# A planned two-layer graph network: leaky rectifier and row scaling to ScalarE, layer-norm scalars to GpSimd, a new table of places

## The chip, the core and the metric

The kernel runs on one core of a Trainium2 chip. The metric is the device time of one execution in microseconds (us); less is better. The core has TensorE (PE in the profile), VectorE (DVE), ScalarE (ACT), GpSimd (POOL) and SyncE (SP), which here issues every DMA. Each engine works through its own list of instructions in the order in which the program gives them, and the engines wait for each other through semaphores.

## The reference

For each of 64 graphs with 256 nodes and 256 features two layers are computed, in f32:

```python
# layer 0: eight heads, four relations
attn = softmax(q @ k^T / sqrt(32))
out  = sum over r of ((attn * (adj == r)) @ (src @ Wv[r] + bv[r]))
x    = LN(src + out @ Wo + bo)
x    = LN(x + gelu(x @ W1 + b1) @ W2 + b2)
# layer 1: two graph-attention steps, then a feed-forward block
e    = leaky_relu(Wh @ a_left + (Wh @ a_right)^T, 0.2)      # 256 x 256
att  = softmax(where(adj > 0, e, -9e15), axis=1)            # over the query nodes
h    = att @ Wh                                             # done twice: W1, a1, then W2, a2
x    = LN(x + h)
x    = LN(x + relu(x @ w_ff1 + b_ff1) @ w_ff2 + b_ff2)
```

LN(v) = (v - mean) / sqrt(var + 1e-5) * gain + shift. There are four layer norms and two graph-attention steps (A and B below) in each graph.

## The kernel before

A graph is cut into 215 named steps (`Graph.operations`). A table `PLACES` gives each a place on a time axis. Graph g's step is emitted at place + 60 g, all steps of all graphs are sorted by that number, and the program is written in this order by hand (`manual_schedule`). So the table decides the order of each engine's list and nothing else: an instruction runs as soon as its engine reaches it and what it waits for has come. About seven graphs are in work at once. In the steady state the order of an engine is read by sorting its steps by their place modulo 60.

The steps that the change and the prediction touch, by name:

- `load`, `xT`, `qk0/1`, `qkc0/1`: the graph's input, the query and key products (PE, line 470) and their copies (ACT).
- `s0/1`, `maxmh`, `expmh`, `recmh`, `nrmmh`: scores (PE, L505), row maximum (DVE, L510), exponential (ACT, L518), reciprocal of its sum (DVE, L523), division by it (ACT, L528), for half m and head h.
- `eTmh`, `eWmh`, `eRmh`: transposition of the weights in 32x32 squares (DVE, L296) and a way through DRAM that puts the squares into place (SP's DMAs, L301 and L305). `ecmh` copies the result to PSUM (ACT, L536), `pmmh` multiplies it with three relation masks (DVE, L540), `plmh` with the fourth (POOL, L545). `v..`, `vc..` are the value products and their bias (PE L489, DVE L496), `po0/1` the products with the masked weights (PE, L557), `oT0/1` their copies (ACT, L563), `wo` and `ya` the output product and its residual.
- `aT aW aR` and `bT bW bR`: the same way through DRAM for the two feed-forward blocks; `hT hW hR` for layer 1's input (L317). `au0..3`, `bu0..3` are the first products (PE, L377), `ax`, `bx` their Gelu and Relu (ACT, L385). The second product is done in seven part products `ad1..7`, `bd1..7` (PE, L412), for which `aS`, `bS` make differences (POOL, L400) and `ae`, `be` add the results to the residual (DVE, L420).
- `st rt nb ln` with 1 to 4: a layer norm. `st` takes mean and variance (DVE, L337 and L339) and adds epsilon to the variance (DVE, L341, tile `ve`). `rt` raises it to the power -1/2 (POOL, L345, tile `rs`). `nb` is -mean * rs (DVE, L349). `ln` applies both (ACT, L354). `lg` and `lb` are gain and shift (POOL, L321 and L324).
- `ga0/1`, `gac0/1`: Wh and the two score vectors (PE L587, ACT L593). Then for A and for B: `ip` spreads the left scores over a PSUM tile (PE, L599), `z` adds the right score as a bias (ACT, L606), `zl` is the leaky rectifier (DVE, L610), `zm` writes the mask (DVE, L613), `zx` is the maximum (DVE, L617), `ze` the exponential and its sum (ACT, L622), `zd` divides Wh's rows by the sum (DVE, L628 for the reciprocal and L630 for two multiplications). `h10/h11` (L636) and `h2` (L650) are the products with the weights, `h1c0/1` their copies (ACT, L642), `h2a` the residual (DVE, L654).

Most matmul results share one PSUM pool with two buffers (`ps_mm`, the tiles that `mm_tile` gives): qk, v, po, wo, ga, ip, h1, h2, au, bu, and the bank of part products 2, 3 and 4. So the second next group of matmuls can't begin before a buffer has been emptied. Part products 1, 5, 6 and 7 of both feed-forward blocks share another single bank. The transposed weights that come back from DRAM have three buffers, the `z` tiles two.

Of the kernel before, what the change touches and what calls it, by code (L numbers as in the profile page):

```python
# [9 lines left out]
F32 = mybir.dt.float32  # L10
# [3 lines left out]
AF = mybir.ActivationFunctionType  # L14
ALU = mybir.AluOpType
AX = mybir.AxisListType

P = 128
S = 32
A = P // S  # L20
EPS = 1e-5
ALPHA = 0.2
# [3 lines left out]

PERIOD = 60.0
PLACES = {
    "load": 40.36, "cast": 58.74, "xT": 60.44, "qk0": 70, "qkc0": 71.44, "qk1": 87.85, "s0": 89.53,
    "qkc1": 91.95, "max01": 94.22, "max03": 94.25, "max02": 94.39, "exp01": 95.36, "rec01": 97.24,  # L30
    "exp03": 106.64, "exp02": 109.12, "jT": 113.27, "max00": 114.1, "exp00": 118.89, "rec02": 119.85,
    "nrm01": 120.5, "rec00": 121.94, "mask0": 122.78, "rec03": 123.27, "eT01": 124.55, "s1": 124.66,
    "mask1": 124.91, "nrm02": 125.88, "max11": 126.34, "v00": 126.75, "nrm03": 126.97, "eT02": 128.02,
    "vc00": 128.34, "nrm00": 128.91, "eW01": 131.85, "eR01": 133.5, "mask2": 134.22, "max13": 137.47,
    "eT03": 137.69, "eW02": 138.09, "max10": 139.15, "exp13": 140.04, "max12": 141.09, "eR02": 141.63,
    "v01": 142.38, "exp11": 142.41, "eT00": 142.98, "exp12": 143.77, "rec11": 143.99, "exp10": 144.12,
    "vc01": 146.63, "rec12": 146.73, "mask3": 146.81, "rec10": 147.48, "nrm11": 148.13, "eW03": 148.24,
    "ec01": 149.05, "eW00": 151.36, "rec13": 152.13, "eT11": 152.55, "nrm12": 153.62, "nrm13": 153.65,
    "eR00": 153.67, "eT12": 155.05, "v10": 155.72, "eW11": 155.83, "y": 156.64, "pm01": 156.67,
    "vc10": 157.33, "ec00": 158.45, "pl00": 159.54, "pl02": 160.62, "pm00": 161.31, "eR03": 162.29,  # L40
    "nrm10": 163.21, "ec02": 163.47, "v11": 164.04, "vc11": 164.08, "mask4": 164.38, "pm02": 164.4,
    "pl01": 165.26, "ec03": 167.13, "eT10": 167.24, "eW12": 168.06, "eR11": 169.25, "pl03": 169.3,
    "pm03": 173.29, "eR12": 174.65, "eW10": 176.2, "eT13": 176.62, "eR10": 177.38, "po0": 181.21,
    "ec11": 181.79, "oT0": 183.85, "pm11": 184.85, "ec10": 187.85, "pl10": 187.87, "pl12": 191.61,
    "pm10": 191.97, "pl11": 192.4, "yb": 193.93, "eW13": 195.61, "eR13": 196.93, "ec12": 197.13,
    "pm12": 199.06, "pl13": 199.85, "ec13": 202.51, "pm13": 205.64, "po1": 215.6, "oT1": 217.97,
    "wo": 219.51, "ya": 223.88, "st1": 228.47, "rt1": 233.65, "nb1": 233.99, "ln1": 238.78, "aT": 240.73,
    "ag": 245.39, "aW": 246.11, "ar": 246.93, "aR": 249.98, "au0": 253.28, "ax0": 255.01, "au1": 255.12,
    "ax1": 256.29, "au2": 257.32, "au3": 258.21, "ax2": 258.83, "ax3": 259.91, "ad1": 260.54, "aS1": 262.22,
    "ae1": 262.56, "ad5": 262.62, "ad2": 263.26, "aS2": 263.54, "aS3": 264.31, "ad3": 264.44, "ad7": 265.04,  # L50
    "aS4": 265.78, "ad4": 265.92, "ad6": 267.49, "ae5": 269.57, "ae7": 270.4, "ae": 270.63, "ae6": 271.84,
    "st2": 272.17, "rt2": 272.17, "nb2": 273.67, "ln2": 274.48, "lg2": 276.04, "lb2": 279.25, "hT": 280.72,
    "hW": 284.48, "hR": 287.09, "ga0": 291.2, "ga1": 292.43, "gac0": 295.5, "gac1": 295.79, "ipA": 296.6,
    "zA": 298, "zlA": 298.97, "zmA": 299.01, "zxA": 299.7, "zeA": 303.47, "zdA": 304.35, "h10": 304.89,
    "h1c0": 305.16, "h11": 306.57, "h1c1": 306.58, "ipB": 307.84, "zB": 308.32, "zlB": 309.79,
    "zmB": 309.85, "zxB": 311.38, "zeB": 311.5, "zdB": 318.17, "h2": 319.09, "h2a": 319.31, "st3": 322.4,
    "rt3": 324.85, "nb3": 325.29, "ln3": 325.64, "bT": 326.01, "bW": 326.15, "bR": 335.32, "bu0": 339.02,
    "bg": 339.45, "bx0": 339.7, "br": 344.42, "bu1": 345.17, "bx1": 346.89, "bu2": 347.56, "bx2": 348.07,
    "bS1": 349.24, "bu3": 349.7, "bd1": 350.78, "bx3": 352.33, "bS2": 355.82, "bd2": 356.22, "bd5": 356.9,
    "bd3": 357.53, "bS4": 358.73, "bd4": 360.41, "be5": 361.74, "be": 361.79, "bS3": 367.41, "bd6": 368.29,  # L60
    "be1": 372.14, "be6": 374.71, "bd7": 376.99, "be7": 378.33, "st4": 407.09, "rt4": 408.17, "nb4": 413.39,
    "ln4": 428.85, "lg4": 434.13, "lb4": 437.94, "store": 455.81,
}
LOAD_PLACE, LOAD_STEP = 62.0, 3.0
FFA_PLACE, GAT_PLACE, FFB_PLACE = 196.0, 200.0, 252.0

# [11 lines left out]
def kernel(  # L80
# [12 lines left out]
    nc = tc.nc  # L93
# [7 lines left out]
    C = N // P  # L101
# [8 lines left out]
    small = ctx.enter_context(tc.tile_pool(name="small", bufs=6))  # L110
# [15 lines left out]
    nhalf = const.tile([P, 2], F32, name="nhalf")  # L126
# [10 lines left out]
    def weight(w, name, mixed=False):  # L137

        k, n = w.shape[0] // P, w.shape[1]
        t = const.tile([P, k, n], F32, name=name)  # L140
        if mixed:
            mixed_rows(t, w)
        else:
            loads.append((t, w.rearrange("(k p) n -> p k n", p=P)))
        return t
# [13 lines left out]
    def rowvec(v, n, name):  # L159
        t = const.tile([P, n], F32, name=name)  # L160
        loads.append((t, _row(v, n)))
        return t
# [30 lines left out]
    scale = 1.0 / math.sqrt(DH)  # L193
# [4 lines left out]
    wo, bo_r = weight(Wo, "wo"), rowvec(bo, D, "bo_r")  # L198
# [127 lines left out]
    class Norm:  # L326
# [5 lines left out]
        def stats(self, y):  # L332
            self.y, name = y, self.name
            st = small.tile([P, C, 6], F32, tag="st", name=f"st_{name}")
            self.mv = small.tile([P, C, 2], F32, tag="mv", name=f"mv_{name}")
            for c in range(C):
                nc.vector.bn_stats(st[:, c, :], y[:, c, :])  # L337
            for c in range(C):
                nc.vector.bn_aggr(self.mv[:, c, :], st[:, c, :])  # L339
            self.ve = small.tile([P, C], F32, tag="ve", name=f"ve_{name}")  # L340
            nc.vector.tensor_scalar(self.ve, self.mv[:, :, 1], EPS, None, op0=ALU.add)  # L341

        def root(self):
            self.rs = small.tile([P, C], F32, tag="rs", name=f"rs_{self.name}")
            nc.gpsimd.tensor_tensor(self.rs, self.ve, nhalf, ALU.pow)  # L345

        def offset(self):
            self.nb = small.tile([P, C], F32, tag="nb", name=f"nb_{self.name}")
            nc.vector.scalar_tensor_tensor(self.nb, self.mv[:, :, 0], -1.0, self.rs, op0=ALU.mult, op1=ALU.mult)  # L349

        def apply(self):
            for c in range(C):
# [69 lines left out]
    class Graph:  # L422
# [179 lines left out]
        def gat_scores(self, right, name):  # L602

            self.z = bp.tile([P, C, N], F32, tag="z", name=f"{name}_z", bufs=2)
            for c in range(C):
                nc.scalar.activation(self.z[:, c, :], self.ps["left"], AF.Identity,  # L606
                                     bias=self.w[:, c, right:right + 1])

        def gat_leaky(self):
            nc.vector.scalar_tensor_tensor(self.z, self.z, ALPHA, self.z, op0=ALU.mult, op1=ALU.max)  # L610

        def gat_mask(self):
            nc.vector.copy_predicated(self.z.rearrange("p c (i n) -> p i c n", i=C), self.no, negc[:, :, None, None].to_broadcast([P, C, C, P]))  # L613
# [11 lines left out]
        def gat_divide(self, cols, name):  # L625

            rden = small.tile([P, C], F32, tag="grden", name=f"{name}_rden")
            nc.vector.reciprocal(rden, self.gden)  # L628
            for c in range(C):
                nc.vector.tensor_scalar(self.w[:, c, :cols], self.w[:, c, :cols], rden[:, c:c + 1], None,  # L630
                                        op0=ALU.mult)

        def second_product(self, ic):
            p = self.ps["h1", ic] = mm_tile([P, D + 2], f"h1_ps{self.g}_{ic}")
# [24 lines left out]
        def operations(self):  # L659

            g, ops = self.g, {}
# [58 lines left out]
            for n, right, name in (("A", D + 2, f"ga{g}"), ("B", D, f"gb{g}")):  # L720
                ops[f"ip{n}"] = lambda right=right, name=name: self.left_product(right + 1, name)
                ops[f"z{n}"] = lambda right=right, name=name: self.gat_scores(right, name)
                ops[f"zl{n}"] = self.gat_leaky
                ops[f"zm{n}"] = self.gat_mask
                ops[f"zx{n}"] = lambda name=name: self.gat_maximum(name)
                ops[f"ze{n}"] = lambda name=name: self.gat_exponential(name)
                ops[f"zd{n}"] = lambda right=right, name=name: self.gat_divide(min(right, D + 2), name)
# [12 lines left out]
    for g in range(B):  # L740
        ops = Graph(g).operations()
# [34 lines left out]
```

## Time and profile before

| | us |
|---|---|
| median of 3 runs | 3729.13 (3727.47 to 3731.34) |
| the profiled execution's own time | 3730.06 |
| its span, first to last instruction | 3728.3 |
| busy: PE, DVE, POOL, ACT | 3525.8, 3253.6, 2683.8, 2476.3 |
| one period of the steady state (one graph in, one graph out) | 56.00 |

The page gives busy times of engines, the groups of instructions with their mean duration in ns and the idle time before them, and the chain of work that ended last: going back from the last instruction, at each step to what released it. A queue that is on this chain sets the time; other idle time costs nothing. The period is read from the chain in order of time, which repeats itself: the part product that follows the two additions on DVE begins at 2025.49 us and again at 2081.49 us.

### The profile page before, as it was taken

What the parts mean: (1) busy time and instruction counts of PE and PEld (TensorE: products, weight loads), DVE (VectorE), ACT (ScalarE), POOL (GpSimd) and SP (SyncE); (2) the same over time, 40 slices, a digit from 0 to 9 for tenths busy, and PEclk for the clock granted to TensorE, in tenths of its full rate; (3) what the DMA queues carried; (4) which work ended last, traced back from release to release, by engine and by line L of the source; (5) the groups of instructions that cost most, each with busy time, mean ns of one, the idle gap of its engine ahead of it and who ended that gap; (6) DMA issues with size and microseconds to landing.
All of it is one profiled execution on the core that took longest, in us unless ns stands there. A gap on an engine that the chain in (4) does not pass through costs nothing.

```text
span 3728.3 us, 72927 instructions
## 1 busy us (share of the span) xinstructions
PE 3525.8 (95%) x25944; PEld 2739.0 (73%) x25944; DVE 3253.6 (87%) x5652; ACT 2476.3 (66%) x6661; POOL 2683.8 (72%) x2246
## 2 busy tenths in 40 slices
PE   5899999999999999999999999999999999999986
PEld 3577777777777777777777777777777777777775
DVE  4789999999999999999999999989989989989963
ACT  4667667667667666666666666666666666666642
POOL 2577777777777777777777777777777777777753
PEclk7999999999999999999999999999999999999998
DMA  6444444444444444444444444444444444444420
GB/s 176 123 127 123 120 132 123 121 131 124 122 131 124 122 131 124 122 131 124 122 131 124 122 129 124 124 128 124 124 128 124 125 128 123 126 128 123 120 77 29
DMA packets 809883, 457.93 MB, mean 123 GB/s; under 512 B 334256, under 2 KB 718896, under 8 KB 809520
## 3 DMA queue, kind: packets, MB, share of 16 engines
q1 hardware_dynamic: 809520, 453.27, 41.5%
q8 instruction: 206, 3.38, 0.4%
q14 instruction: 157, 1.29, 0.1%
HBM read 243.42 MB, written 201.33 MB: 119 GB/s over the span
## 4 chain that ended last, share of the span: by engine, by line
PE 77%; DVE 16%; ACT 2%; DMA 2%; issue 1%; SPq 1%; POOL 0%; ACTq 0%; POOLq 0%; DVEq 0%
PE po L557 12%; PE ffb_ps L377 11%; PE v_ps L489 9%; PE ffa_ps L377 6%; PE ffa_po L412 5%; PE ffb_po L412 5%; PE ffa_pq L412 5%; PE ffb_pq L412 4%; PE s L505 4%; PE h_ps L636 4%; PE ga_wps L587 3%; PE h_ps L650 3%; DVE pm L540 3%; PE qk_ps L470 3%; PE wo_ps L577 3%; DVE gb_z L610 3%
## 5 line engine op out<-in xcount | busy, mean ns | idle before, releaser
L540 DVE TENSOR_TENSOR pm<-rel,pe 128x1536 f32<-128x1536 uint8 x512 | 886.6, 1732 | 9.8 <-ACT pe L536 7.7
L545 POOL TENSOR_TENSOR pl<-rell,eT 128x512 f32<-128x512 bf16 x512 | 589.4, 1167 | 117.9 <-DMA eT<-eT_d 98.9
L345 POOL TENSOR_TENSOR rs_x<-ve_x,nhalf 128x2 f32<-128x2 f32 x256 | 182.5, 713 | 550.4 <-DVE ve_x L341 549.9
L489 PE MATMUL v_ps<-wv,xT 128*128 128x512 f32 x1024 | 491.3, 602 | 0.4 <-DVE v L496 0.4
L518 ACT ACTIVATE e<-s,nmax 128x256 f32<-128x256 f32 x1024 | 473.1, 477 | 20.8 <-DVE nmax L510 12.7
L377 PEld LDWEIGHTS ffb_ps<-ffb_T,f 128*128 128x128 f32 x2048 | 391.3, 191 | 121.6 <-issue 71.6
L377 PE MATMUL ffb_ps<-ffb_T,f 128*128 128x256 f32 x2048 | 466.7, 381 | 13.8 <-DMA ffb_T<-ffb_T_d 13.8
L377 PE MATMUL ffa_ps<-ffa_T,w 128*128 128x256 f32 x2048 | 466.5, 381 | 1.5 <-ACT ffa_h L385 1.5
L528 ACT ACTIVATE e<-e,rden 128x256 f32<-128x256 f32 x1024 | 457.1, 507 | 8.7 <-DVE rden L523 8.7
L377 PEld LDWEIGHTS ffa_ps<-ffa_T,w 128*128 128x128 f32 x2048 | 386.4, 191 | 52.5 <-ACT ffa_h L385 2.1
L557 PE MATMUL po<-pm,v 128*32 128x256 f32 x6144 | 366.3, 385 | 18.4 <-DVE pm L540 18.4
L536 ACT COPY pe<-eT 128x512 f32<-128x512 f32 x512 | 307.0, 600 | 113.6 <-DVE rden L523 93.9
L385 ACT ACTIVATE ffb_h<-ffb_ps,bf_c 128x256 f32<-128x256 f32 x512 | 215.1, 471 | 239.2 <-PE ffb_ps L377 239.2
L296 DVE STREAM_TRANSPOSE eT_sq<-e 128x512 f32<-128x512 f32 x512 | 358.2, 700 | 12.0 <-DMA eT_d<-eT_sq 10.9
L510 DVE TENSOR_REDUCE nmax<-s 128x2 f32<-128x512 f32 x512 | 336.8, 679 | 7.2 <-PE s L505 7.2
L462 POOL TENSOR_SCALAR rel<-adT 128x512 uint8<-128x512 bf16 x192 | 310.1, 1624 | 0.0
L557 PEld LDWEIGHTS po<-pm,v 128*32 128x32 f32 x6144 | 188.5, 110 | 164.0 <-issue 25.2
L385 ACT ACTIVATE ffa_h<-ffa_ps,b_c 128x256 f32<-128x256 f32 x512 | 208.0, 473 | 144.4 <-PE ffa_ps L377 124.0
L489 PEld LDWEIGHTS v_ps<-wv,xT 128*128 128x128 f32 x1024 | 185.5, 191 | 159.6 <-issue 151.5
L400 POOL TENSOR_TENSOR ffa_t<-ffa_h,ffa_t 128x512 f32<-128x512 f32 x128 | 162.9, 1272 | 178.1 <-ACT ffa_h L385 178.1
L496 DVE TENSOR_TENSOR v<-v_ps,bv_r 128x512 f32<-128x512 f32 x256 | 173.4, 677 | 65.4 <-PE v_ps L489 65.3
L420 DVE TENSOR_TENSOR ffa_res<-ffa_po,ffa_res 128x256 f32<-128x256 f32 (+2 forms) x256 | 134.2, 524 | 91.4 <-PE ffa_po L412 86.8
(141 smaller groups left out, 8054.4 us busy)
## 6 DMA issues: line engine op xcount, KB each, us to landing
eT_d<-eT_sq SPq DMA_DIRECT2D x512, 256.0 KB, 3.1
eT<-eT_d SPq DMA_DIRECT2D x512, 256.0 KB, 2.9
xin<-in_x_dram SPq DMA_DIRECT2D x256, 64.0 KB, 3.4
adi<-in_adj_dram SPq DMA_DIRECT2D x64, 256.0 KB, 3.1
y<-in_x_dram SPq DMA_DIRECT2D x64, 256.0 KB, 4.4
ffa_T_d<-ffa_T_sq SPq DMA_DIRECT2D x64, 256.0 KB, 2.0
ffa_T<-ffa_T_d SPq DMA_DIRECT2D x64, 256.0 KB, 2.7
hT_d<-hT_sq SPq DMA_DIRECT2D x64, 256.0 KB, 3.1
```

The costliest lines, as they stand in the source:

```text
L296: nc.vector.transpose(self.sq.rearrange("p a c k y -> p (c k) a y"), src.rearrange("p c (k a x) -> p (c k) a x", k=KD, a=A))
L377: nc.tensor.matmul(p[:, f - f0, :], self.wa[:, k, f * P:(f + 1) * P], self.x.nodes(k), start=(k == 0), stop=(k == KD - 1))
L385: nc.scalar.activation(self.h[half][:, f1 + f, :], self.ps[f0][:, f, :], self.func, bias=self.ba[:, f0 + f:f0 + f + 1])
L412: nc.tensor.matmul(self.p[bank][:, k], a[:, f], seven[self.name[:3]][i][:, f], start=(f == 0), stop=(f == KF // 2 - 1))
L462: nc.gpsimd.tensor_scalar(t.rearrange("p b c k y -> p (c k) b y"), self.adT.rearrange("p c k (b y) -> p (c k) b y", b=A), float(r), None, ...
L489: nc.tensor.matmul(p, self.xT[:, k, jc * P:(jc + 1) * P], wv[:, k, m].rearrange("p r n -> p (r n)"), start=(k == 0), stop=(k == KD - 1))
L510: nc.vector.tensor_reduce(self.nmax[m, h], self.s4[m][h].rearrange("p (c n) -> p c n", c=C), AX.X, ALU.max, negate=True)
L518: nc.scalar.activation(e[:, ic, :], self.s4[m][h][:, ic * N:(ic + 1) * N], AF.Exp, bias=self.nmax[m, h][:, ic:ic + 1], accum_out=self.den[ ...
L528: nc.scalar.activation(e[:, ic, :], e[:, ic, :], AF.Copy, scale=self.rden[m, h][:, ic:ic + 1])
L540: nc.vector.tensor_tensor(self.pm[m, h], self.rel.rearrange("p r b c k y -> p r (b c k y)"), bc(self.pe[m, h], [P, R - 1, C * N]), ALU.mult)
L545: nc.gpsimd.tensor_tensor(self.pm_l[m, h], self.rel_l.rearrange("p b c k y -> p (b c k y)"), self.et[m, h].t.rearrange("p b c k y -> p (b ...
L557: nc.tensor.matmul(po[hp, :], self.v[m][:, jc, r, hp], w, start=(r == 0 and jc == 0), stop=(r == R - 1 and jc == C - 1))
```

## The change

The leaky rectifier of both graph-attention steps becomes ScalarE's function Prelu with a slope of 0.2, in the instruction that added the bias; the steps `zlA` and `zlB` are gone, which leaves 213 names. The multiplications of `zd` go from DVE to ACT; its reciprocal stays on DVE. In the layer norms the addition of epsilon moves from `st` on DVE to `rt` on POOL, and `nb` from one instruction on DVE to two on POOL. All places are new, the loading of the weights included; the period of the table stays 60.

```diff
 PLACES = {
...
 }
-LOAD_PLACE, LOAD_STEP = 62.0, 3.0
-FFA_PLACE, GAT_PLACE, FFB_PLACE = 196.0, 200.0, 252.0
+LOAD_PLACE, LOAD_STEP = 122.0, 3.0
+FFA_PLACE, GAT_PLACE, FFB_PLACE = 255.0, 262.0, 264.0
...
                 nc.vector.bn_aggr(self.mv[:, c, :], st[:, c, :])
-            self.ve = small.tile([P, C], F32, tag="ve", name=f"ve_{name}")
-            nc.vector.tensor_scalar(self.ve, self.mv[:, :, 1], EPS, None, op0=ALU.add)
 
         def root(self):
             self.rs = small.tile([P, C], F32, tag="rs", name=f"rs_{self.name}")
-            nc.gpsimd.tensor_tensor(self.rs, self.ve, nhalf, ALU.pow)
+            nc.gpsimd.tensor_scalar(self.rs, self.mv[:, :, 1], EPS, None, op0=ALU.add)
+            nc.gpsimd.tensor_tensor(self.rs, self.rs, nhalf, ALU.pow)
 
         def offset(self):
             self.nb = small.tile([P, C], F32, tag="nb", name=f"nb_{self.name}")
-            nc.vector.scalar_tensor_tensor(self.nb, self.mv[:, :, 0], -1.0, self.rs, op0=ALU.mult, op1=ALU.mult)
+            nc.gpsimd.tensor_tensor(self.nb, self.mv[:, :, 0], self.rs, ALU.mult)
+            nc.gpsimd.tensor_scalar(self.nb, self.nb, -1.0, None, op0=ALU.mult)
...
-                nc.scalar.activation(self.z[:, c, :], self.ps["left"], AF.Identity,
+                nc.scalar.activation(self.z[:, c, :], self.ps["left"], AF.Prelu, alpha=ALPHA,
                                      bias=self.w[:, c, right:right + 1])
-
-        def gat_leaky(self):
-            nc.vector.scalar_tensor_tensor(self.z, self.z, ALPHA, self.z, op0=ALU.mult, op1=ALU.max)
...
             for c in range(C):
-                nc.vector.tensor_scalar(self.w[:, c, :cols], self.w[:, c, :cols], rden[:, c:c + 1], None,
-                                        op0=ALU.mult)
+                nc.scalar.activation(self.w[:, c, :cols], self.w[:, c, :cols], AF.Copy, scale=rden[:, c:c + 1])
```

The steady order that the two tables give on the engines, sorted by place modulo 60 (before begins at `po0`, after at `h2`; DVE and ACT only in the stretches that the prediction reads):

```
PE before:  po0 s1 h10 h11 v00 ipB bd6 qk0 au0 au1 bd7 au2 au3 h2 ad1 v01 ad5 ad2 ad3 ad7 ad4 ad6 qk1 s0 po1
            v10 bu0 wo v11 bu1 bu2 bu3 bd1 ga0 ga1 bd2 ipA bd5 bd3 bd4
PE after:   h2 ad1 v01 qk1 ad5 ad2 ad3 ad6 ad4 ad7 v10 po1 s0 v11 bu0 wo bu1 bu2 bu3 bd1 ga0 ga1 bd5 ipA
            bd2 bd3 po0 bd4 v00 h10 s1 h11 bd6 ipB qk0 au0 au1 bd7 au2 au3
DVE before: zlB zmB zxB pm10 be1 be6 | h2a max12 st3 ae1
DVE after:  be5 max11 zmB zxB be6 | h2a st3 ae1 vc01 | ae6 ae rec11 rec12 ae5 ae7 st2 rec10 eT11 pm01 vc10 vc11
            hT pm02 ya max00 st4 pm00 st1 pm03 eT10 eT12 max01 max02 be1 zmA zxA aT max03 eT13 zdA(reciprocal)
ACT after:  ln2 oT1 | nrm12 nrm10 ec00 bx1 nrm13 exp00 bx2 ec03 bx3 gac0 gac1 ln1 zA exp01 exp02 zeA zdA oT0
            exp03 | h1c0 nrm01 h1c1 nrm02 zB nrm00 qkc0 zeB ax0 ec10 ax1 zdB ax2
POOL after: rt2 nb2 lg2 lb2 pl02 pl01 pl00 mask0 bg br bS1 rt4 pl03 rt1 nb1
SP after:   eW03 eR03 eW11 hW hR eR11
```

| distance in the table | before | after |
|---|---|---|
| `load` to `qk0` | 29.6 | 50.4 |
| `qk0` to `bd7`, the last PE step | 307.0 | 305.6 |
| `bd7` to `store` | 78.8 | 88.8 |

## The prediction

> **What bounds the kernel now.** First the page: span and busy times.
>
> ```profile
> span 3728.3 us, 72927 instructions
> PE 3525.8 (95%) x25944; PEld 2739.0 (73%) x25944; DVE 3253.6 (87%) x5652; ACT 2476.3 (66%) x6661; POOL 2683.8 (72%) x2246
> ```
>
> PE is busiest, but DVE is near it. Then the windows of two neighbouring periods, to see whether the state is steady (columns: window, length, busy us of PE, PEld, DVE, ACT, POOL, clock):
>
> ```profile
> 2024.79:2080.79 56.00, 54.32 (x404) 42.36 (x404) 50.82 (x89) 38.55 (x105) 41.97 (x35) 1.00 0.42 125
> 2080.79:2136.79 56.00, 54.32 (x404) 42.36 (x404) 50.93 (x89) 38.56 (x105) 41.98 (x35) 1.00 0.43 126
> ```
>
> It repeats every 56.00 us at full clock. Then the chain in order of time (start, us, what), where PE loses its lead once a period:
>
> ```profile
> 2072.35 1.72 PE v_ps L489 x4
> 2074.06 0.23 PE gb_ips L599 x2
> ...
> 2074.38 0.85 ACT gb_z L606 x2
> ...
> 2075.25 1.70 DVE gb_z L610
> ...
> 2076.97 0.81 DVE gb_z L613
> ...
> 2077.80 0.69 DVE gb_max L617
> 2078.49 1.66 DVE pm L540
> 2080.15 0.61 DVE ffb_res L420
> ...
> 2080.79 0.57 DVE ffb_res L420
> ...
> 2081.49 1.13 PE ffb_po L412 x8
> ```
>
> After `ipB` ends at 2074.29, PE has bd6 (0.89), qk0 and au0, au1 (1.73 each) = 6.08 us to do and would begin `bd7` at 2080.37. It begins at 2081.49, since DVE, one instruction after another, does the leaky rectifier, mask, maximum, an unrelated 1.66 us product and only then the additions on which bd7 waits. The waits confirm both places where DVE holds PE (total us, times, longest):
>
> ```profile
> PE ffb_po L412 <- DVE ffb_res L420: 72.7, 62, 3.6
> PE ffa_po L412 <- DVE ffa_res L420: 36.7, 63, 1.8
> ```
>
> These are 1.13 us before bd7 and 0.54 us before `ad5` in the period's timeline. Each restart costs 0.24 more (the first group of eight takes 1.13 instead of 0.89). So PE's own work is 56.00 - 1.13 - 0.54 - 0.48 = 53.85 us a graph: all that a relieved DVE could give is 2.15 us, or 3.8%.
>
> **What the Trainium skill says.** "SBUF — State Buffer", Who interferes with whom: a DVE instruction with two SBUF inputs, or a tensor_scalar in a two-port mode, shares its port with GpSimd, and the later one waits. The trace agrees: the same rectifier takes 692 to 1696 ns, the 128x2 `nb` 145 to 1223, the row scaling 340 to 1469. "ScalarE: Activation LUTs", Table sets: cheap functions are in every set; Prelu is not named there. The trace has two loads a graph, for Gelu and for Exp, and none for Identity, Copy or Relu; no run here shows Prelu. "ScalarE activation tables: per-element evaluation and per-set limits", What a function is on this engine: the table read doesn't change an instruction's cost. Gelu and Relu at 473 and 471 ns (L385) agree.
>
> **The change part by part**, for one graph. The groups that give the prices (count, then busy us and mean ns); the A forms of L610 and L630 have 1032 and 850 ns, the epsilon at L341 273:
>
> ```profile
> L610 DVE SCALAR_TENSOR_TENSOR gb_z<-gb_z 128x512 f32<-128x512 f32 x64 | 102.7, 1605 | 39.9 <-ACT gb_z L606 39.9
> L630 DVE TENSOR_SCALAR gb_wh<-gb_wh,gb_rden 128x256 f32<-128x256 f32 x128 | 110.2, 900 | 2.3
> L349 DVE SCALAR_TENSOR_TENSOR nb_x<-mv_x,rs_x 128x2 f32<-128x2 f32 x256 | 150.1, 586 | 22.9 <-POOL rs_x L345 19.4
> L345 POOL TENSOR_TENSOR rs_x<-ve_x,nhalf 128x2 f32<-128x2 f32 x256 | 182.5, 713 | 550.4 <-DVE ve_x L341 549.9
> L528 ACT ACTIVATE e<-e,rden 128x256 f32<-128x256 f32 x1024 | 457.1, 507 | 8.7 <-DVE rden L523 8.7
> ```
>
> *Rectifier into Prelu.* DVE loses 1605 + 1032 ns = 2.64 us. ACT's four instructions stay; 0.47 us each as now (L606). Bounds: 0, and four table loads of 1283 ns (5.13 us) if Prelu were not in Exp's set. I take 0. Nothing below 0, since the operands are the same.
>
> *Row scaling.* DVE loses 2 x 900 + 2 x 850 = 3.50 us; ACT gains four instructions of the kind of L528, 4 x 0.507 = 2.0 us. The new wait is ACT's, in order, for DVE's reciprocal; behind it in A stands `oT0`, on which a PSUM buffer depends, in B `ax2`. Cover in A, from ipA to h10: bd2, bd3, bd4, po0, v00 = 7.98 us, against z 0.85, exp01 and exp02 1.8, zeA 1.1, reciprocal 0.15, scaling 0.9, hops 0.4 = 5.2. In B, from ipB to h2: 9.54 against 6.0 to the end of ax0 (worked out below), ec10 0.6, ax1 0.85, scaling 0.9 = 8.4. So it costs nothing; without the 2.8 and 1.1 to spare, its 0.9 would come out on PE each time.
>
> *Norm scalars.* DVE loses four times 273 (ve) and 586 (nb) ns = 3.44 us. POOL gets twelve 128x2 instructions that no row shows. Bounds: 0.10 us (the 128x1 memset) and 0.713 (the power). The cast of 128x512 takes 612 ns, and memsets of 1 and 128 elements (99, 205 ns) give 0.83 ns an element, so 612 - 427 leaves 0.19 fixed. I take 0.2, so 2.4 us (1.2 to 8.6). A gain of POOL is possible only where DVE held its port: L321 takes 1.69 us beside the B rectifier and 1.28 elsewhere, 0.4 a graph.
>
> *Sums.* DVE 50.9 - 9.6 = 41.3; ACT 38.6 + 2.0 = 40.6; POOL 42.0 + 2.4 - 0.4 = 44.0. All are far under PE's 53.85, so what remains are waits in the new order. I lay PE's groups end to end with the chain's durations and ask of each whether its supplier is in time.
>
> *Old stall, bd7.* Cover after ipB: qk0, au0, au1 = 5.19 us. Chain: z 0.85, mask 0.81, maximum 0.69, be6 0.57, hops 0.3 = 3.2. It goes, with 2.0 to spare. *Old stall, ad5.* Cover after h2: ad1 0.89, v01 1.72, qk1 1.73 = 4.34. Chain: h2a 0.69, st3 0.89, ae1 0.70, hops 0.3 = 2.6. It goes.
>
> *Next late, po0.* It needs the PSUM buffer that zA empties; zA stands behind ln1 on ACT, ln1 waits for nb1 on POOL, and POOL's list from rt2 to nb1 runs without a gap. From the end of ad7 the cover is v10 1.72, po1 3.59, s0 1.08, v11 1.72, five groups of 1.73 (bu0, wo, bu1, bu2, bu3), bd1 0.89, ga 1.76, bd5 0.89, ipA 0.22, bd2 and bd3 1.78 = 22.3 us. The chain: additions and st2 on DVE 3.2; rt2 0.92, nb2 0.4; ln2 1.1; lg2, lb2 2.55; pl02, pl01, pl00 3.4; mask0 1.7; bg, br, bS1 3.9; rt4 0.92; pl03 1.15; rt1 0.92; nb1 0.4; ln1 1.1, zA 0.85; hops 0.4 = 22.9. Wait 0.6, with restart 0.8. Seven of the new small instructions lie on it, so each 0.1 us in their price is 0.7 here.
>
> *Next late, au2.* It needs the buffer that ax0 empties. Cover after ipB: qk0, au0, au1, bd7 = 6.08. Chain on ACT: z 0.85, mask and maximum 1.5, zeB 1.1, table load 1.28, ax0 0.85, hops 0.4 = 6.0, and up to 0.4 if nrm00 and qkc0 finish after the maximum. I take 0.2, with restart 0.4.
>
> *DMAs and queues.* SP's reads now stand close behind their writes. hW stands behind eR03 and eW11; hT to ga0 needs the write's 3.1 and the read's 3.7 us (DMA table), 6.8; hT ends about one us after vc11, and from there to ga0 are wo, bu1..3, bd1, about 8. `bg` on POOL takes over the residual buffer that `store` of two graphs before reads, 2.8 after it in the table (3.6 before), and a store lands after 3.5. I take 0.2 for all small ones (0 to 1.0). v11 needs oT1 behind ln2: cover 6.39 from ad7, chain 3.2 + 1.3 + 1.1 + 0.4 + 0.3 = 6.3; nothing, but no spare.
>
> Period: 53.85 + 0.8 + 0.4 + 0.2 = 55.25, 0.75 less. The steady pattern runs from about 178 to 3540 us, 60 periods: -45 us. Fill and drain: from qk0 to bd7 the two tables have the same length, the head and tail where they grow are idle waits in the table alone; weights come later relative to the graph. I take +5 (-10 to +15). Span 3728.3 - 45 + 5 = 3688. Around it lie 3730.06 - 3728.3 = 1.8 us: 3690. The profiled execution is 0.9 us over the median of the runs, which I leave in.
>
> **The rivals.** *All of the gain* (0.2): small POOL instructions cost 0.1 (0.7 less at po0, which ends that wait) and the ACT waits vanish: 54.05 a period, -117 + 5: about 3618. For it: DVE, which made both stalls, gets 9.6 us of air. Against it: the sums at po0 and au2 have no spare.
>
> *POOL in the norms becomes the wait* (0.25, the slower side). If a small instruction on POOL costs 0.4 with its hand-over to the next, po0 waits 1.4 more: 56.65, +39 + 5, about 3774. It decides from 0.31 each, where the 0.75 is eaten. For it: each is dependent on the one before; the pair lg2, lb2 starts 1.37 apart where independent neighbours start 1.23 apart, so a dependent start may cost another 0.1. Against it: 0.19 fixed by the cast. At the upper bound, 0.713, it would be 58.8, or 3905; I hold that for very unlikely, as the power itself must account for most of that row.
>
> *Prelu needs its own table* (0.03): the B chain to au2 gets two loads, 2.57, zA one, 1.28: 59.1, about 3921.
>
> *The gain is given back exactly* (0.1): the new waits sum to 2.1, within 0.2% of 3729, which is about what a measurement of this kernel can tell from no change.
>
> **How the numbers follow.** Forecast (0.42): 54.6 to 55.8 a period, 3651 to 3721. Faster by over 0.2%: 0.42 + 0.2 = 0.62; within 0.2%: 0.10; slower: 0.25 + 0.03 = 0.28. The range leaves out a tenth at each side: half of the full-gain case below 3620, and above 3780 the costlier half of the POOL case and the tables. Within the faster side alone it is 3620 to 3721.
>
> **What would show it.** Right: no L610, no L341 on DVE; DVE near 41 us a period; the waits of L412 on DVE gone; a period near 55.2 with PE waiting at L557 for ACT's zA and at L377 for ACT. The small POOL rows decide between the first two rivals. Wrong: PE idle behind DMA reads of hT or the transposed weights, or a slower fill, or more than two table loads a graph.

## The result and the profile after

The changed kernel takes 3729.1 us (median of 12 runs, 3721.65 to 3738.93) against 3728.97 (12 runs, 3727.47 to 3731.43) before: ratio 1.0001, 95% interval 0.9992 to 1.0010. A change that took 8.8 us of work a graph off the second busiest engine (3253.6 - 2691.9 us over 64 graphs; the forecast was 9.6) moved nothing. The page of the profiled execution (3735.23 us, so one of the longer runs):

```profile
span 3733.5 us, 72960 instructions
PE 3527.7 (94%) x25944; PEld 2767.2 (74%) x25944; DVE 2691.9 (72%) x4756; ACT 2560.1 (69%) x6917; POOL 2796.0 (75%) x3014
```

DVE fell from 87% to 72% as planned, but PE's idle time did not shrink (202.5 us of the span before, 205.8 after). Two neighbouring periods in windows (window, length, busy us of PE, PEld, DVE, ACT, POOL, clock, DMA share, GB/s):

```profile
2006.55:2062.01 55.46, 54.19 (x405) 42.65 (x405) 41.49 (x75) 39.86 (x108) 43.30 (x48) 1.00 0.43 127
2062.01:2117.61 55.60, 54.19 (x404) 42.65 (x405) 42.02 (x75) 39.85 (x108) 43.81 (x48) 1.00 0.43 126
```

A period takes 55.5 instead of 56.0. What PE waits for (total us, times, longest):

```profile
PE ga_wps L590 <- DMA hT<-hT_d: 110.0, 64, 9.0
...
PE ffb_po L415 <- DVE ffb_res L423: 4.2, 2, 3.0
...
PE ffa_po L415 <- DVE ffa_res L423: 3.2, 2, 1.6
```

Both old stalls are gone (72.7 and 36.7 us before); in their place stands one new wait in every graph, for the DMA that brings layer 1's input. The chain at the end of a period:

```profile
2110.13 3.38 PE ffb_ps L380 x16
2113.51 3.96 DMA hT<-hT_d
...
2117.61 1.99 PE ga_wps L590 x8
```

And why this DMA is late: DVE's transposition hT, POOL's products `pl02 pl01 pl00` and SP's list in the same period, from three timelines (start, us):

```profile
2107.32 0.70 DVE L299 STREAM_TRANSPOSE hT_sq<-ffa_res 128x512 f32<-128x512 f32 x1
```

```profile
2107.00 3.42 POOL L548 TENSOR_TENSOR pl<-rell,eT 128x512 f32<-128x512 bf16 x3
```

```profile
2100.92 0.47 SPq L304 DMA_DIRECT2D eT_d<-eT_sq  x1
2109.31 0.36 SPq L308 DMA_DIRECT2D eT<-eT_d  x1
2109.78 0.44 SPq L304 DMA_DIRECT2D eT_d<-eT_sq  x1
2110.26 0.43 SPq L304 DMA_DIRECT2D hT_d<-hT_sq  x1
2113.51 0.67 SPq L320 DMA_DIRECT2D hT<-hT_d  x1
```

hT is done at 2108.02. Its write hW stands third in SP's list. First comes eR03, which reads the weights of head 3 back and needs one of three buffers; it goes at 2109.31, when the second of POOL's three products is done. hW goes at 2110.26, 2.24 us after hT (the same in nearly every period), and lands 3.25 later, with two other transfers in flight beside it. Only then may the read go.

The prices of the new instructions (group, count, busy us, mean ns, idle before):

```profile
L347 POOL TENSOR_TENSOR rs_x<-rs_x,nhalf 128x2 f32<-128x2 f32 x256 | 183.7, 718 | 21.3
L352 POOL TENSOR_SCALAR nb_x<-nb_x 128x2 f32<-128x2 f32 x256 | 61.6, 240 | 22.4
L630 ACT ACTIVATE ga_wh<-ga_wh,ga_rden 128x258 f32<-128x258 f32 x128 | 58.3, 503 | 39.8 <-DVE ga_rden L628 39.8
L346 POOL TENSOR_SCALAR rs_x<-mv_x 128x2 f32<-128x2 f32 x256 | 57.1, 223 | 125.6 <-DVE rden L526 75.6 <-DVE mv_x L342 39.4
L609 ACT ACTIVATE gb_z<-gb_ips,gb_wh 128x256 f32<-128x256 f32 x128 | 53.7, 470 | 3.7 <-PE gb_ips L602 3.7
L351 POOL TENSOR_TENSOR nb_x<-mv_x,rs_x 128x2 f32<-128x2 f32 x256 | 50.3, 197 | 15.1
```

**Where the rest of the gain went.** I took the 64 starts of ga0 from both traces. The median of the 63 periods between them is 55.66 us (56.00 before), but eleven are over 0.6 longer than that, 16.9 us together; before, none is. Ten of the eleven are five pairs. In the first of a pair hW's write takes 3.95 to 5.73 us instead of 3.3 and ga0 starts late (7.4 us in all five); in the second PE works for a while at half its clock (8.8 us, see the last section). Why these five writes are slow isn't shown. From the 6th to the 58th period the mean is 55.95 us for 56.01 before, so in the steady state the gain is gone. From the first ga0 to the last it is 3505.2 us (165.39 to 3670.56) for 3511.6 (156.97 to 3668.60) before, so the periods give -6.5 in all. The first ga0 comes later, and what follows the last one is longer. The tile's answers, before and after (ns, then the first start and that of the last matmul, which is ga1's, in us):

```profile
L587 PE MATMUL ga_wps<-gext,hT x512: 382/382/772, 157.0 to 3670.2; 128*128 128x260 f32 x171
```

```profile
L590 PE MATMUL ga_wps<-gext,hT x512: 382/383/773, 165.4 to 3673.7; 128*128 128x260 f32 x171
```

Filling +8.4, periods -6.5, emptying +3.2: together the +5 us of this execution.

### The profile page after: what moved, and what is told of

The parts are those of the page before. It is cut to its first block, busy times and chain, and to the rows that moved or that the text cites. A ratio compares the mean times of both kernels' runs of the same rounds, so it can differ in the third digit from the quotient of the medians.

```text
span 3733.5 us, 72960 instructions
## 1 busy us (share of the span) xinstructions
PE 3527.7 (94%) x25944; PEld 2767.2 (74%) x25944; DVE 2691.9 (72%) x4756; ACT 2560.1 (69%) x6917; POOL 2796.0 (75%) x3014
## 4 chain that ended last, share of the span: by engine, by line
PE 77%; DMA 10%; POOL 4%; DVE 3%; issue 2%; ACT 2%; SPq 2%; POOLq 0%; ACTq 0%; DVEq 0%
PE ffa_ps L380 11%; PE po L560 10%; PE v_ps L492 9%; DMA hT<-hT_d 7%; PE ffa_po L415 6%; PE qk_ps L473 6%; PE ffb_ps L380 5%; PE ffb_pq L415 5%; PE ffb_po L415 5%; PE ffa_pq L415 5%; PE ga_wps L590 4%; PE h_ps L635 3%; PE h_ps L649 3%; PE s L508 3%; DMA hT_d<-hT_sq 3%
## 5 line engine op out<-in xcount | busy, mean ns | idle before, releaser
L380 PEld LDWEIGHTS ffb_ps<-ffb_T,f 128*128 128x128 f32 x2048 | 390.4, 191 | 95.3 <-issue 43.8
L380 PEld LDWEIGHTS ffa_ps<-ffa_T,w 128*128 128x128 f32 x2048 | 383.7, 190 | 55.8 <-ACT ffa_h L388 6.3
L560 PE MATMUL po<-pm,v 128*32 128x256 f32 x6144 | 364.3, 385 | 18.5 <-DVE pm L543 17.9
L299 DVE STREAM_TRANSPOSE eT_sq<-e 128x512 f32<-128x512 f32 x512 | 350.3, 694 | 16.5 <-DMA eT_d<-eT_sq 14.4
L403 POOL TENSOR_TENSOR ffa_t<-ffa_h 128x512 f32<-128x512 f32 x64 | 81.8, 1278 | 371.6 <-ACT ffa_h L388 371.6
L539 ACT COPY pe<-eT 128x512 f32<-128x512 f32 x512 | 304.8, 595 | 41.5 <-DVE pm L543 19.0
L560 PEld LDWEIGHTS po<-pm,v 128*32 128x32 f32 x6144 | 188.0, 111 | 190.3 <-issue 51.8
L357 ACT ACTIVATE ffa_res<-ffa_res,nb_x,rs_x 128x256 f32<-128x256 f32 x256 | 139.8, 593 | 238.7 <-POOL nb_x L352 238.7
L465 POOL TENSOR_SCALAR rel<-adT 128x512 uint8<-128x512 bf16 x192 | 289.0, 1506 | 12.0 <-DMA adT<-adb 12.0
L492 PEld LDWEIGHTS v_ps<-wv,xT 128*128 128x128 f32 x1024 | 175.4, 191 | 151.7 <-issue 124.6
L423 DVE TENSOR_TENSOR ffb_res<-ffb_po,ffb_res 128x256 f32<-128x256 f32 (+2 forms) x256 | 133.2, 521 | 207.6 <-PE ffb_po L415 140.1
L590 PE MATMUL ga_wps<-gext,hT 128*128 128x260 f32 x512 | 138.2, 416 | 110.0 <-DMA hT<-hT_d 110.0
```

What stands on the lines that cost most here:

```text
L299: nc.vector.transpose(self.sq.rearrange("p a c k y -> p (c k) a y"), src.rearrange("p c (k a x) -> p (c k) a x", k=KD, a=A))
L380: nc.tensor.matmul(p[:, f - f0, :], self.wa[:, k, f * P:(f + 1) * P], self.x.nodes(k), start=(k == 0), stop=(k == KD - 1))
L465: nc.gpsimd.tensor_scalar(t.rearrange("p b c k y -> p (c k) b y"), self.adT.rearrange("p c k (b y) -> p (c k) b y", b=A), float(r), None, ...
L492: nc.tensor.matmul(p, self.xT[:, k, jc * P:(jc + 1) * P], wv[:, k, m].rearrange("p r n -> p (r n)"), start=(k == 0), stop=(k == KD - 1))
L539: nc.scalar.copy(self.pe[m, h], self.et[m, h].t.rearrange("p b c k y -> p (b c k y)"))
L560: nc.tensor.matmul(po[hp, :], self.v[m][:, jc, r, hp], w, start=(r == 0 and jc == 0), stop=(r == R - 1 and jc == C - 1))
```

## The experiments

**One place on SP.** In the changed kernel:

```diff
-    "hW": 321.721,
+    "hW": 320.0,
```

> The changed kernel with one place moved: hW, the write of layer 1's input to DRAM, goes ahead of eR03 and eW11 on SP (321.721 becomes 320.0). Theory A: in the changed kernel hW stands 2.24 us behind the end of hT because SP waits at eR03 for a buffer that pl01 frees, and PE's wait of 1.7 us before ga0 hangs on that alone. Then hW starts within 0.1 us of hT, PE's waits at ga0 shrink from 110 us to under 20, and some 1.6 us in each of 60 periods come off: about 3635. Rival B: the norm chain on POOL or the buffer behind zA, zeB and ax0 is next and nearly as late, so that the period only falls to 55.2 and the time to about 3700, with PE waiting at L560 or L380 for ACT. Rival C: the write lands later because it now meets the other transfers; then the time stays within 0.3% of the changed kernel.

Measured 3656.84 us, ratio to before 0.9801 (0.9787 to 0.9816). hW now starts 0.03 us after hT and lands in 2.3 us; PE's wait at ga0 fell to 11.6 us. Theory A has the cause, and rival B what comes next, though it costs less than B said (a period of 55.2):

```profile
PE po L560 <- ACT ga_z L609: 31.7, 58, 0.6
```

```profile
2078.65 0.26 POOL nb_x L352
2078.94 1.09 ACT y L357 x2
2080.03 0.73 ACT ga_z L609 x2
2080.80 3.66 PE po L560 x64
```

This is the path that the prediction worked out for po0: nb1 on POOL, ln1, zA, then PE. The period is 54.73.

**The same cause by another way.** The order stays as changed, but the buffer for which eR03 waits is there:

```diff
-            self.et[m, h] = Transposed(f"eT{self.g}_{m}_{h}", ap, "eT", 3)
+            self.et[m, h] = Transposed(f"eT{self.g}_{m}_{h}", ap, "eT", 4)
```

> The changed kernel with its places, but four instead of three buffers for the transposed weights that come back from DRAM. Theory A: hW stands behind eR03 on SP, and eR03 waits for a buffer that pl01 on POOL frees; with a fourth buffer eR03 goes at once, hW starts within 0.3 us of hT although the order is unchanged, and the time comes near the kernel with hW moved: 3650 to 3670. Rival B: what delays hW is something else in SP's list (the wait for eW03's landing, or the issue of two more transfers): 3700 or more.

3652.04 us, 0.9791 (0.9774 to 0.9807). hW starts 0.03 us after hT and lands in 2.1. So it was the buffer that POOL frees late, met in SP's order, and neither the issuing itself nor the landing of eW03.

**More of the suspected wait.** In the changed kernel:

```diff
-"eR11": 205.899,
+"eR11": 201.3,
```

> The changed kernel with eR11 put ahead of hW on SP (205.899 becomes 201.3), so that hW has to wait in addition until eW11's write has landed, about 2.3 us more. Theory A (PE hangs on hW's start): the period grows by nearly all of it, 2.0 to 2.5 us, so about 3850 to 3880. Rival B (the wait before ga0 is what is left over from another limit): under 1 us a period, below 3790.

4064.97 us, 1.0899 (1.0881 to 1.0917): theory A's direction, more than twice its size.

```profile
PE ga_wps L590 <- DMA hT<-hT_d: 289.4, 64, 11.9
```

The wait grew by 2.8 us a graph, the period by 5.6 (61.30). The rest is PE's clock: in the chain ga0 and ga1 take 3.80 us instead of 1.99, and the group after them 1.62 to 1.71 instead of 0.89 (more of this in the last section).

**The POOL list in front of po0.** On top of the moved hW:

```diff
-"mask0": 141.136,
+"mask0": 152.0,
```

> The kernel with hW moved, and mask0 on POOL moved behind bS4 (141.136 becomes 152.0), which takes 1.5 us out of POOL's list between lb2 and nb1. Theory A: what holds PE before po0 in the kernel with hW moved (31.7 us in 58 waits for zA, and a restart of 0.24 each) is the POOL list that leads to nb1, ln1 and zA; then these waits go, the period falls from 54.73 to 53.9 to 54.1, and the time to 3605 to 3620. Rival B: another supplier is as late (ax0 before au2, oT1 before v11); then PE waits at L380 or L492 for ACT and the time stays over 3635.

3609.11 us, 0.9675 (0.9661 to 0.9690), as theory A said: no wait at L560 for zA is left, the period is 53.96.

**Both moves and the fourth buffer,** in the changed kernel:

```diff
-"mask0": 141.136,
+"mask0": 152.0,
...
-"hW": 321.721,
+"hW": 320.0,
...
-            self.et[m, h] = Transposed(f"eT{self.g}_{m}_{h}", ap, "eT", 3)
+            self.et[m, h] = Transposed(f"eT{self.g}_{m}_{h}", ap, "eT", 4)
```

> The kernel with hW and mask0 moved, and four buffers for the transposed weights. Theory A: its period, 53.96 us, is PE's own work (53.85 by the sum), so a further buffer has nothing to give but a little in the filling: 3600 to 3612. Rival B: the odd longer periods that are left there (54.1 to 54.4) come from SP's waits for these buffers; then they go and 5 us or more with them, below 3603.

3606.54 us, 0.9669 (0.9653 to 0.9685), as theory A said, and the fastest here, 3.3% below both kernels. Rival B is right that the longer periods (up to 54.41 with the two moves) go with the buffer, the longest being 53.99 now; but they were worth only some 2 us. The window over ten periods says why no further wait can be removed:

```profile
2000.00:2539.60 539.60, 539.60 (x4044) 425.86 (x4040) 416.88 (x741) 399.14 (x1080) 435.89 (x471) 1.00 0.44 130
```

PE is busy in all of it.

**New instructions, old places.** The changed instructions with the table of before; of the table only this differs from the kernel before:

```diff
-"zlA": 298.97,
-"zlB": 309.79,
```

> All the changed instructions, with the places of the kernel before (zlA and zlB left out). Theory A: the old table has no DMA wait before ga0, and the rectifier's 1.7 us leave the chain between ipB and bd7, so the stall before bd7 (1.13 and 0.24) goes and the one before ad5 stays: 54.6 a period, about 3645. Rival B: the old table puts the norms and the row scaling where ACT and POOL are late; then PE gets new waits and the time is between 3700 and 3760.

3695.76 us, 0.9905 (0.9890 to 0.9920), just below rival B's range. The stall before bd7 went, as theory A said, and a new wait for POOL came, as rival B said:

```profile
PE ffb_pq L412 <- POOL ffb_t L400: 47.3, 58, 0.8
PE ffa_po L412 <- DVE ffa_res L420: 23.1, 63, 1.6
```

**Old instructions, new places.** The instructions of before under the table of after, with the rectifier given a place just behind its `z`:

```diff
+"zlA": 329.7,
+"zlB": 345.1,
```

> The instructions of before with the new places (zlA and zlB put back right behind zA and zB). Theory A: the new table relies on DVE being free; with 9.6 us more on DVE the path to hT gets later (the rectifier, the scaling and two small instructions of the norm come into DVE's list) and PE waits more before ga0: 57 to 58.5 a period, 3800 to 3880. Rival B: the new order alone has removed the two old stalls and the old instructions fit as well; then it is within 0.5% of the changed kernel.

4040.18 us, 1.0833 (1.0817 to 1.0849): worse than theory A's 3800 to 3880. The largest wait isn't at ga0 but before ad5, for DVE:

```profile
PE ffa_po L415 <- DVE ffa_res L423: 137.6, 63, 3.8
PE ga_wps L590 <- DMA hT<-hT_d: 79.8, 64, 8.5
```

The three parts were then tried alone, in the kernel before with its own table.

**The rectifier alone:**

```diff
-                nc.scalar.activation(self.z[:, c, :], self.ps["left"], AF.Identity,
+                nc.scalar.activation(self.z[:, c, :], self.ps["left"], AF.Prelu, alpha=ALPHA,
...
-        def gat_leaky(self):
-            nc.vector.scalar_tensor_tensor(self.z, self.z, ALPHA, self.z, op0=ALU.mult, op1=ALU.max)
```

> The kernel before with its places; only the leaky rectifier goes into ScalarE's instruction, zlA and zlB are gone. Theory A: the chain from ipB to bd7 loses 1.7 us, so the wait before bd7 (1.13) and its restart (0.24) go, while the 0.54 and 0.24 before ad5 stay: 54.6 a period, about 3645. Rival B: other DVE work that stood behind the rectifier is late all the same (the two additions come behind a 1.66 us product): then at most half of it goes, 3690 or more.

3642.27 us, 0.9762 (0.9748 to 0.9777), as theory A said. Period 54.53; what is left is the other old stall:

```profile
PE ffa_po L412 <- DVE ffa_res L420: 36.8, 63, 1.8
```

**The row scaling alone:**

```diff
-                nc.vector.tensor_scalar(self.w[:, c, :cols], self.w[:, c, :cols], rden[:, c:c + 1], None,
-                                        op0=ALU.mult)
+                nc.scalar.activation(self.w[:, c, :cols], self.w[:, c, :cols], AF.Copy, scale=rden[:, c:c + 1])
```

> The kernel before with its places; only the row scaling of both graph-attention steps goes from DVE to ACT. Theory A: DVE's scaling stands behind neither of the two old stalls (in the period's timeline it lies after bd7's additions, and DVE idles 0.7 us before h2a), so 3.5 us less on DVE change nothing: within 0.3% of 3729. Rival B: ACT, which waits for the reciprocal in front of other work, delays ax2 or ec12 and PE loses 0.3 us or more a period: 3745 or more.

3723.38 us, 0.9982 (0.9974 to 0.9990): 6 us less, close to nothing, as theory A said.

**Rectifier and scaling,** the last two diffs together:

> The kernel before with its places, with the rectifier in ScalarE's instruction and the row scaling on ACT, the norms as before. Theory A: the rectifier alone gives the gain (3642), the scaling nothing, and the 54 us that the kernel with all three new parts and old places loses against that are the norms' on POOL: 3635 to 3650. Rival B: the scaling on ACT costs a part of the 54 us: 3660 or more.

3639.75 us, 0.9758 (0.9744 to 0.9773), as theory A said.

**The norms' scalars alone:**

```diff
-            nc.vector.tensor_scalar(self.ve, self.mv[:, :, 1], EPS, None, op0=ALU.add)
-            nc.gpsimd.tensor_tensor(self.rs, self.ve, nhalf, ALU.pow)
+            nc.gpsimd.tensor_scalar(self.rs, self.mv[:, :, 1], EPS, None, op0=ALU.add)
+            nc.gpsimd.tensor_tensor(self.rs, self.rs, nhalf, ALU.pow)
...
-            nc.vector.scalar_tensor_tensor(self.nb, self.mv[:, :, 0], -1.0, self.rs, op0=ALU.mult, op1=ALU.mult)
+            nc.gpsimd.tensor_tensor(self.nb, self.mv[:, :, 0], self.rs, ALU.mult)
+            nc.gpsimd.tensor_scalar(self.nb, self.nb, -1.0, None, op0=ALU.mult)
```

> The kernel before with its places; only epsilon and offset of the layer norms go to POOL. Theory A: POOL's list from st4 to the difference that ffb_pq needs gets longer (in the kernel with all new instructions and old places PE waits 47.3 us there), and neither of the two old stalls is helped: 0.5 to 1.0 more a period, 3760 to 3790. Rival B: DVE is relieved by 3.4 us, of which most was waiting for the shared port, and that pays for it: 3730 or less.

3807.71 us, 1.0208 (1.0191 to 1.0225): theory A's side, 18 us over its upper end.

```profile
PE ffb_po L412 <- DVE ffb_res L420: 78.6, 62, 3.0
PE ffb_pq L412 <- POOL ffb_t L400: 66.8, 58, 1.2
```

The old stall before bd7 stays whole, and the one at ffb_pq is added: there POOL's list holds two norms between the difference products (read from the table; not tried apart). With all three parts and old places the same norms cost 3695.76 - 3639.75 = 56 us, alone 77.

**The norms back on DVE, in the new order with hW moved:** the last diff in reverse, in the changed kernel, and

```diff
-"hW": 321.721,
+"hW": 320.0,
```

> The kernel with hW moved, but epsilon and offset of the layer norms as in the kernel before (on DVE). Theory A: the seven small POOL instructions of 0.2 us and their hand-overs of about 0.07 leave the list that leads to zA; the wait before po0 (0.55 and a restart of 0.24) goes: 3605 to 3625. Rival B: DVE, with 3.4 us more, is later with st2, hT or the additions; PE then waits before ga0 or ad5 and the time is 3657 or more.

3867.73 us, 1.0366 (1.0351 to 1.0382). Theory A is wrong here, by some 250 us, and rival B is right: PE waits before ad5, and the wait before po0 grew to 77.1 us instead of going.

```profile
PE ffa_po L415 <- DVE ffa_res L423: 137.8, 63, 3.8
```

`nb` on DVE needs POOL's power, and the new table has the power far down in POOL's list. DVE's and POOL's timelines:

```profile
2047.41 0.34 DVE L344 TENSOR_SCALAR ve_x<-mv_x 128x2 f32<-128x2 f32 x1
2049.90 1.21 DVE L352 SCALAR_TENSOR_TENSOR nb_x<-mv_x,rs_x 128x2 f32<-128x2 f32 x1 [2.15 <-POOL rs_x L348]
2051.03 0.68 DVE L423 TENSOR_TENSOR ffa_res<-ffa_po,ffa_res 128x512 f32<-128x512 f32 x1
```

```profile
2047.70 1.48 POOL L465 TENSOR_SCALAR rel<-adT 128x512 uint8<-128x512 bf16 x1
2049.15 0.72 POOL L348 TENSOR_TENSOR rs_x<-ve_x,nhalf 128x2 f32<-128x2 f32 x1
```

DVE stands for 2.15 us, then needs 1.21 for two elements while POOL works, and behind it is ae1, on which ad5 waits on PE. The old instructions in the new places share this, with 188.9 us in 130 waits of DVE for `rs` for the 189.2 in 130 here: the new table presupposes a DVE that never waits for POOL's scalars.

## Why the prediction was wrong, point by point

*What bounds.* Right. PE's own work was put at 53.85 us a graph; 53.96 is reached when nothing is late. The gain was there to be had: 3606.54 us.

*Prices.* Right. Prelu costs what Identity cost, 470 ns, and its table loads number 64 before Gelu and 62 before Exp as ever, which the Trainium skill, "ScalarE: Activation LUTs", Table sets, doesn't promise for Prelu by name; the rival with four loads is out. Scaling 503 to 519 ns for 507. A small POOL instruction 197, 223 and 240 ns for the 200 chosen between 100 and 713. DVE 41.5 to 42.0 us a period for 41.3, ACT 39.9 for 40.6, POOL 43.3 to 43.8 for 44.0.

*Old stalls.* Right, both gone. The rectifier alone gave back 1.47 us a period where 1.37 stood at bd7.

*po0.* Right in place and nearly in size: 0.55 a wait and a restart of 0.24 when hW is out of the way, for the predicted 0.8. In the changed kernel itself it doesn't show, since PE has just waited longer in front of it.

*au2.* Predicted 0.4; no trace of it once the rest was cleared. Its sum (6.0 against 6.08) was right to within a tenth, and I took the wrong side.

*Scaling "costs nothing".* Right: 6 us less alone.

*The step that failed* is "DMAs and queues": "I take 0.2 for all small ones (0 to 1.0)". It named hW behind eR03 and eW11, set 6.8 us of DMA time against a cover of about 8, and charged no time for what eR03 itself waits for. The cover was right: with hW moved, ga0 starts 8.01 us after hT's end. The chain was not 6.8 but 2.24 + 3.25 + 4.10 = 9.6: 2.24 us of standing behind eR03, whose buffer depends on a POOL product that the prediction had in another sum, then the write in 3.25 us for 3.1 and the read in 4.10 for 3.7. So the sizes of the transfers were nearly right, and the term that was put at nothing was the standing. The wait of 1.5 and its restart of 0.24 are 1.7 us a period where 0.2 stood, and the eleven longer periods add 0.3 on average. In the kernel before, where PE waited for DVE and not for this DMA, no period was over 0.6 longer than the median.

*Why the period looks nearly right.* 53.96 + 1.7 is 55.66, the measured median, and inside the forecast 54.6 to 55.8. That is luck: 1.2 us charged for po0 and au2 didn't come, and hid most of the 1.5 missing at ga0. The longer periods and the filling then carried the time out of the range. The prediction had named PE idle behind the reads of hT, and a slower fill, as signs of being wrong; both came. Its rival with the gain given back exactly (0.1) has the right time, but it named no wait that would do it.

*Fill and drain* was mis-sized: +5 taken, +11.6 measured in that execution. Of the 8.4 at the start 3.7 go with hW (first ga0 at 161.7 us instead of 165.4), and with the old places the new instructions alone account for 3.1 (160.1). With the fourth buffer, in the changed order, all but 1.1 goes (158.0), and from the last ga0 to the end it is 58.7 us instead of 62.9 (59.7 before). So most of the 11.6 goes with one more buffer; by which waits wasn't traced.

*The slower rival* (POOL in the norms) had the right danger and the wrong condition. Not the price of one small instruction decided, which was 0.2, but where the norms stand in POOL's list: alone in the old table they cost 2.1%.

So the result of no difference is a sum whose parts the experiments separate, each where it was tried. In the old order the rectifier takes off 88 us and the scaling 2 to 6, and the norms put 56 back. The new order frees both old stalls and takes off another 39 (3695.76 to 3656.84) when hW has its better place, and loses 72 again (3656.84 to 3729.1) by one place on SP, or one buffer too few.

## What to carry to other kernels

When work leaves a busy engine, the next limit can be a queue's order instead of an engine's load: for each transfer on the path, walk the issuing queue backwards and ask of every entry in front of it what that entry waits for, a free buffer included. A path through a DMA needs more spare time than its median: here five slow writes of 64 cost 16 us, late starts and clock together, while in the kernel before, writes of up to 4.9 us lengthened no period by more than 0.4. And where several small changes are joined with a new order, try each alone: here one of three carried nearly all of the gain, and one was a loss where it stood.

## What the runs showed of the hardware that was not expected

PE's clock drops when it waits long. The Trainium skill, "TensorE: Matmul & The Clock Gate", Part 1, says that after an idle window of about 3.4 us the array runs at half rate until it has been busy about as long. The traces agree on the half rate, but here shorter waits were enough. In the changed kernel PE usually idles 1.5 us before ga0 and the group takes 1.99 us. After the five slow writes it idled 2.19, 2.61, 3.06, 3.23 and 3.64 us, and each time the granted clock was 0.5 for 3.4 or 6.8 us; after one wait of 2.16 us it stayed at 1. The shortest of the five, and the clock just after it (window, length, busy us, clock, DMA share, GB/s):

```profile
443.75 3.60 PE L590 MATMUL ga_wps<-gext,hT 128*128 128x260 f32 x8 [2.19 <-DMA hT<-hT_d]
```

```profile
444.00:447.00 3.00, 3.00 (x8) 2.30 (x8) 1.19 (x3) 0.38 (x1) 2.76 (x5) 0.50 0.56 196
```

And the longest, after a write of 5.7 us:

```profile
2175.43 3.81 PE L590 MATMUL ga_wps<-gext,hT 128*128 128x260 f32 x8 [3.64 <-DMA hT<-hT_d]
```

```profile
2173.00:2188.00 15.00, 12.56 (x107) 10.01 (x108) 6.59 (x14) 7.34 (x24) 8.24 (x11) 0.77 0.40 110
```

The mean granted clock is 0.77 in that longer window. With eR11 moved forward PE idles 4.5 us on average in each period, and the mean clock of the whole run is 0.937 instead of 0.982. So a wait of 1.5 us costs 1.7 and one of 4.5 costs some 7 (61.30 - 53.96). Between them lie the five slow writes: starts that were 0.7 to 2.2 us late cost another 1.3 to 2.9 us each by the clock.

A write of 256 KB from SBUF to DRAM landed in 2.1 to 2.3 us when no other was issued within a microsecond of it, and in 3.3 behind two others issued within a microsecond; both are typical values of the same step, in kernels that differ in its place or in the buffer for which the entry ahead of it waits.
